# A recommender forward pass: the token sum and the comparison constant move into a PSUM bank, and the table sums into one bank with pairs that end at step ends

## Chip, cores, metric

The kernel runs on one core of one Trainium2 chip. The metric is device time in microseconds (us), lower is better. In the profile PE is TensorE's matmuls, PEld its weight loads, DVE is VectorE, ACT is ScalarE, POOL is GpSimd.

## What is computed

```python
tok = word_emb[token_idx].mean(axis=1)        # (16384, 32) indices, 50000 x 300 table
e1 = emb_mh1[mh1_idx].mean(axis=1)            # 20 indices each; 1000, 5000, 10000 rows x 64
e2 = emb_mh2[mh2_idx].mean(axis=1)
e3 = emb_mh3[mh3_idx].mean(axis=1)
o1, o2, o3, o4 = emb_oh1[oh1_idx], ...        # one index each; 100, 50, 20, 1000 rows
emb = concatenate([tok, e1, e2, e3, o1, o2, o3, o4], axis=1)      # 748 columns
wide = sums of one-column tables at the same small-table indices
h = relu(emb @ W1 + b1)                       # 1024
h = relu(h @ W2 + b2)                         # 512
h = relu(h @ W3 + b3)                         # 256
return sigmoid(h @ Wd + bd + wide)
```

All data is f32; the batch is 16384.

## The kernel before

The batch is cut into 128 tiles of 128 examples; four tiles make a block of 512, on which the layers run (the last four tiles form blocks of two, one and one). A tile passes through three pieces of work, and the loop at L454 writes their order out by hand, in 11 steps (STEPS) per tile, with the program's own order kept on each engine.

**Tokens** (L212). For each of 32 tokens GpSimd issues one indirect DMA (a gather) that brings 128 rows of 300 f32 values into SBUF. Four gathers make a group; the ring holds three groups. One group later (TOK_LAG) `add_up` (L204) has VectorE reduce the four rows and the running sum, five rows of 300, to the next group's running sum or, at the end of the tile, to the feature tile g.

**Small tables** (L281 to L345). The rows of the seven small tables lie in SBUF as three bf16 terms, in 138 slices of 128 rows. A lookup becomes a count matrix: VectorE compares the row number and the slice number of each lookup with the constant `iota` (`one_hots`, L289, two comparisons a step, for six examples of each half, in the last step four), TensorE multiplies the two one-hot matrices into counts (`counts`, L307, 12 small matmuls into pc), and ScalarE writes them to cnt as fp8 (L314). In the next tile's steps `small_sums` multiplies cnt by the terms, 138 matmuls of 195 columns into pg (L332), two tables to a pg tile, four such pairs; after each pair VectorE reduces the three terms into g (L339). pg has two PSUM buffers.

**Layers** (L367 to L419). For a whole block TensorE transposes the features in six chunks (L374), VectorE scales them into x (L375), and 88 f32 matmuls (L384) with ScalarE's relu (L393) make the three layers; then the output row (L409, L413, L417). This runs beside the next block's tiles.

Each piece is a generator. `Paced` (L421) takes an equal part of its units in each step: the sums a part of 138 + LULL units, the layers a part of a block's units over the next block's steps, a chunk of transposes counting two (CHUNK_WORK) and a matmul one. Within a step the order is: comparisons of the next step, counts, tokens, table sums, layers. The key transposes (L272, L275) come once a block. In the first tile the tables are converted to bf16 terms (L154 to L172), by ScalarE and by VectorE's L169.

Of the kernel before, what the change touches and what calls it, by code (L numbers as in the profile page):

```python
# [8 lines left out]
F32 = mybir.dt.float32  # L9
# [10 lines left out]
N_MH, EMB = 20, 64  # L20
ROW = EMB + 1
D1, D2, D3 = 1024, 512, 256
TOK_GROUP = 4
TOK_LAG = 1
TOK_RING = 3
BLOCK = 512
HALF = P // 2
N_SMALL = 3 * N_MH + 4
ONEHOT = 6
STEPS = -(-HALF // ONEHOT)  # L30
LULL = 12
CHUNK_WORK = 2

# [11 lines left out]
def kernel(  # L47
# [31 lines left out]
        slices[f] = (n_h, n_h + n)  # L79
        n_h += n  # L80

    tokp = ctx.enter_context(tc.tile_pool(name="tok", bufs=1))
    const = ctx.enter_context(tc.tile_pool(name="const", bufs=1))
    idxp = ctx.enter_context(tc.tile_pool(name="idx", bufs=2))
    keyp = ctx.enter_context(tc.tile_pool(name="keys", bufs=1))
# [5 lines left out]
    xp = ctx.enter_context(tc.tile_pool(name="x", bufs=1))  # L91
    ps_h = ctx.enter_context(tc.tile_pool(name="ps_h", bufs=2, space=bass.MemoryType.PSUM))
    ps_c = ctx.enter_context(tc.tile_pool(name="ps_c", bufs=1, space=bass.MemoryType.PSUM))
    ps_g = ctx.enter_context(tc.tile_pool(name="ps_g", bufs=2, space=bass.MemoryType.PSUM))

# [20 lines left out]
    nc.vector.memset(scale[0:EMB, 4:5], 1.0 / N_MH)  # L118


    iota_i = keyp.tile([P, n_h], I32, name="iota_i", tag="low")
    nc.gpsimd.iota(iota_i, pattern=[[1, n_h]], base=0, channel_multiplier=0)
    iota = const.tile([P, n_h], BF16, name="iota")
    nc.vector.tensor_copy(iota, iota_i)

    first = const.tile([P, 2, N_SMALL], I32, name="first")
    lookups = [("e1", N_MH), ("e2", N_MH), ("e3", N_MH), ("o1", 1), ("o2", 1), ("o3", 1), ("o4", 1)]
# [65 lines left out]
        for sb, dram in ((wd_sb, wd), (b1_sb, b1), (b2_sb, b2), (b3_sb, b3), (bd_sb, bd)):  # L193
            nc.sync.dma_start(out=sb, in_=dram)

    GROUP_ROWS = 1 + TOK_GROUP
    ring = tokp.tile([P, TOK_RING * GROUP_ROWS, TOK_D], F32, name="ring")
    n_groups = N_TOK // TOK_GROUP  # L200
    under_way = []
    features = {}

    def add_up(t, q):  # L204

        n = t * n_groups + q
        row, next_row = (k % TOK_RING * GROUP_ROWS for k in (n, n + 1))
        to = features[t][:, 0:TOK_D] if q == n_groups - 1 else ring[:, next_row, :]
        rows = ring[:, row + (q == 0) : row + GROUP_ROWS, :]
        nc.vector.tensor_reduce(to, rows.rearrange("p t d -> p d t"), AX.X, ALU.add)  # L210

    def tokens(t, it):  # L212


        for q in range(n_groups):
            row = 1 + (t * n_groups + q) % TOK_RING * GROUP_ROWS
            for r in range(TOK_GROUP):
                j = q * TOK_GROUP + r
                nc.gpsimd.indirect_dma_start(  # L219
                    out=ring[:, row + r, :],  # L220
                    out_offset=None,
                    in_=word,
                    in_offset=bass.IndirectOffsetOnAxis(ap=it[:, j : j + 1], axis=0),
                )
            under_way.append((t, q))
            if len(under_way) > TOK_LAG:
                add_up(*under_way.pop(0))
            yield 1
# [23 lines left out]
    def lookup_keys(ix):  # L252

        pairs = NSUB // 2
        low = keyp.tile([P, pairs, 2, N_SMALL], I32, name="low", tag="low")
        nc.vector.tensor_single_scalar(low, ix, P - 1, op=ALU.bitwise_and)
        nc.vector.tensor_single_scalar(ix, ix, 7, op=ALU.logical_shift_right)
        keys = keyp.tile([P, pairs, 2, 2 * N_SMALL], BF16, name="keys")
        for r in range(pairs):
            view = keys[:, r].rearrange("p w (f c) -> p w f c", f=2)  # L260
            nc.vector.tensor_copy(view[:, 0], low[:, r])
            nc.vector.tensor_add(view[:, 1], ix[:, r], first)
        return keys
# [58 lines left out]
    def small_sums(g, cnt):  # L322


        by_slice = cnt.rearrange("l f p h -> l (f p) h")
        for i in (0, 2, 6, 4):
            pair = SMALL[i : i + 2]
            pg = ps_g.tile([P, 2, 3 * ROW], F32, name="pg")
            for j, f in enumerate(pair):
                h0, h1 = slices[f]  # L330
                for h in range(h0, h1):
                    nc.tensor.matmul(  # L332
                        pg[:, j, :], by_slice[:, :, h], terms[:, h, :], start=(h == h0), stop=(h == h1 - 1)
                    )
                    if h < h1 - 1:
                        yield 1
            at = TOK_D + i * ROW
            n = len(pair)
            nc.vector.tensor_reduce(  # L339
                g[:, at : at + n * ROW].rearrange("p (f d) -> p f d", f=n),  # L340
                pg[:, 0:n, :].rearrange("p f (c d) -> p f d c", c=3),
                AX.X,
                ALU.add,
            )
            yield n if i != 6 else n + LULL  # L345

    def wide_term(g):
        wide = wp.tile([P, 1], F32, name="wide")
# [47 lines left out]
    def mlp(b0, gs, wides):  # L396

        n = len(wides) * P
        x = xp.tile([P, NK, BLOCK], F32, name="x", tag="even")
        yield from transposed(x, gs)  # L400
        h1 = xp.tile([P, M1, BLOCK], F32, name="h1", tag="odd")
        yield from layer(h1, w1_sb, b1_sb, x, chunk_k, M1, n)
        h2 = xp.tile([P, M2, BLOCK], F32, name="h2", tag="even")
        yield from layer(h2, w2_sb, b2_sb, h1, [P] * M1, M2, n)
        h3 = xp.tile([P, M3 + 1, BLOCK], F32, name="h3", tag="odd")
        yield from layer(h3, w3_sb, b3_sb, h2, [P] * M2, M3, n)
        po = ps_h.tile([1, BLOCK], F32, name="po", tag="ph")
        for k in range(M3):
            nc.tensor.matmul(  # L409
                po[:, 0:n], wd_sb[:, k : k + 1], h3[:, k, 0:n], start=(k == 0), stop=False  # L410
            )
        for s, wide in enumerate(wides):
            nc.tensor.matmul(  # L413
                po[:, s * P : (s + 1) * P], wide, ident, start=False, stop=(s == len(wides) - 1)
            )
        y = h3[0:1, M3, 0:n]
        nc.scalar.activation(y, po[:, 0:n], AF.Sigmoid, bias=bd_sb)  # L417
        nc.sync.dma_start(out=out[b0 : b0 + n, :].rearrange("n o -> o n"), in_=y)
        yield M3  # L419

    class Paced:  # L421


        def __init__(self, gen, size, n):
            self.gen, self.size, self.n = gen, size, n
            self.done = self.part = 0

        def go(self):
            self.part += 1
            while self.done * self.n < self.size * self.part:  # L430
                work = next(self.gen, None)
                if work is None:
                    return
                self.done += work

        def finish(self):
            for _ in self.gen:
                pass

    tiles = B // P
    mlp_size = NK * (CHUNK_WORK + M1) + M1 * M2 + M2 * M3 + M3
    ctx.enter_context(tc.manual_schedule())
    sizes = [NSUB] * (tiles // NSUB - 1) + [NSUB - 2, 1, 1]
    it, ix = load_indices(0)
# [5 lines left out]
    for t in range(tiles + 1):  # L454
        s = t % NSUB
        sums = None
        if before:
            features[t - 1] = g = gp.tile([P, G_COLS], F32, name="g")
            sums = Paced(small_sums(g, before), n_h + LULL, STEPS)
        if t < tiles:  # L460
            if s == 0 and t:
                it, sc = next_it, next_sc
            cnt = cp.tile([P, 2, HALF, n_h], FP8, name="cnt", tag="counts")
            toks = Paced(tokens(t, it[:, s, :].bitcast(U32)), n_groups, STEPS)
        else:
            last_tokens()
        for i in range(STEPS):
            if t < tiles:
                hot_now = hot
                if s == 1 and i == 0 and t + NSUB < tiles:  # L470
                    next_it, ix = load_indices(t // NSUB + 1)
                if s == 2 and i == 0 and t + NSUB < tiles + 1:
                    next_keys = lookup_keys(ix)
                if i < STEPS - 1:
                    hot = one_hots(sc, s, i + 1)
                elif t + 1 < tiles:
                    hot = one_hots(next_sc if s == NSUB - 1 else sc, (s + 1) % NSUB, 0)
                counts(cnt, hot_now, i)
                if t == 0 and i % 3:
                    next(tables_on_chip, None)  # L480
                if t == 0 and i == STEPS - 1:
                    load_weights()
                toks.go()
            if s == 2 and i == 1 and t + NSUB < tiles + 1:
                next_sc = key_columns(next_keys)
            if sums:
                sums.go()
            if layers:
                layers.go()
        if before:  # L490
            sums.finish()
            gs.append(g)
            wides.append(wide_term(g))
        before = cnt if t < tiles else None
        if t == 0:
            for _ in tables_on_chip:
                pass
        if len(gs) == sizes[0]:
            if layers:
                layers.finish()  # L500
            steps = STEPS * (sizes[1] if len(sizes) > 1 else 1)
            layers = Paced(mlp(b0, gs, wides), mlp_size, steps)
            b0 += len(gs) * P
            gs, wides, sizes = [], [], sizes[1:]
    layers.finish()
# [39 lines left out]
```

## Time and profile before

| | us |
|---|---|
| median of 3 timed runs | 5522.64 (5520.22 to 5526.17) |
| the profiled execution | 5520.13 |
| its span | 5518.2 |
| TensorE matmul busy | 5127.8 |
| VectorE busy | 4677.3 |
| GpSimd busy | 4111.8 |
| ScalarE busy | 2544.8 |

The span is the time from the first to the last instruction of the profiled execution. A group's row gives line, engine, operation, output and inputs with shapes, count, then busy us, mean ns of one, and the idle time of the engine just before these instructions with what ended most of it. A row of the timeline gives start, duration, engine, line, operation and, in brackets, the idle time before it and what ended it; in the chain of waits a row is start, length, engine, tile, line and count.

### The profile page before, as it was taken

Reading aid. Unit: us, or ns where it says so; the run is one execution under the profiler, and the core shown is the slowest. Engines: PE = TensorE matmul, PEld = TensorE weight load, DVE = VectorE, ACT = ScalarE, POOL = GpSimd, SP = SyncE. Lnnn points to the kernel's source line nnn. Section 1 sums busy time; section 2 is a strip of 40 time slices with the busy share of each in tenths; the row PEclk is TensorE's granted clock in tenths of the full one; section 3 lists DMA queues with packets and bytes.
Section 4 is the critical chain, followed back from the end, with each engine's and each line's share of the span. In section 5 each row is a group of like instructions: output and inputs, shape, how many; then the busy total and the mean of one; then the engine's idle time right before and its main releaser. Section 6 shows DMA issues by size and latency. Waiting matters only on the chain.

```text
span 5518.2 us, 98099 instructions
## 1 busy us (share of the span) xinstructions
PE 5127.8 (93%) x41320; PEld 3192.2 (58%) x41320; DVE 4677.3 (85%) x5069; ACT 2544.8 (46%) x2000; POOL 4111.8 (75%) x4103
## 2 busy tenths in 40 slices
PE   3699999999999999999999999999999999999999
PEld 2555555555555555556555555555565555565558
DVE  7888888888888888888888888888888888888863
ACT  4344444444444444444444444444444444444443
POOL 5777777777777777777777777777777777777762
PEclk9799999999999999999999999999999999999999
DMA  5444444444444444444444444444444444444431
GB/s 161 118 120 118 121 118 120 122 118 119 121 120 121 121 119 119 121 119 121 120 120 121 119 120 121 120 119 120 121 119 122 119 119 120 120 121 120 119 97 36
DMA packets 245306, 652.21 MB, mean 118 GB/s; under 512 B 108977, under 2 KB 111988, under 8 KB 244863
## 3 DMA queue, kind: packets, MB, share of 16 engines
q0 software_dynamic: 196608, 629.41, 41.5%
q1 hardware_dynamic: 48255, 16.53, 1.3%
q8 instruction: 323, 5.29, 0.4%
q14 instruction: 120, 0.98, 0.1%
HBM read 645.59 MB, written 0.07 MB: 117 GB/s over the span
## 4 chain that ended last, share of the span: by engine, by line
PE 63%; POOL 12%; DVE 11%; issue 10%; DMA 4%; DVEq 0%; ACT 0%; POOLq 0%
PE ph L384 33%; PE pg L332 21%; POOL ring L219 12%; PE pc L307 8%; DMA ring<-in_word_emb_dram,it 4%; DVE ring L210 4%; DVE row L289 2%; DVE slice L289 1%; DVE x L375 1%; PE po L409 1%; DVE g L339 1%; DVE sc L275 1%; DVE g L210 1%; PE po L413 0%; PE pt L374 0%
## 5 line engine op out<-in xcount | busy, mean ns | idle before, releaser
L219 POOL DMA_INDIRECT ring<-in_word_emb_dram,it x4096 | 4110.9, 1004 | 1320.3 <-issue 1118.9
L314 ACT ACTIVATE cnt<-pc 128x1656 fp8e3<-128x1656 f32 (+1 forms) x1408 | 2121.8, 1507 | 2232.7 <-PE pc L307 2208.4
L210 DVE TENSOR_REDUCE ring<-ring 128x300 f32<-128x1500 f32 (+1 forms) x896 | 2510.2, 2802 | 207.8 <-DMA ring<-in_word_emb_dram,it 205.2
L332 PE MATMUL pg<-terms,cnt 128*128 128x195 bf16 x17664 | 1874.9, 256 | 93.4 <-DVE g L339 93.4
L332 PEld LDWEIGHTS <-cnt 128*128 128x128 fp8e3 x17664 | 1614.6, 145 | 251.8 <-issue 101.6
L384 PE MATMUL ph<-x,w_sb 128*128 128x512 f32 (+5 forms) x3264 | 1470.7, 580 | 42.2 <-DVE sc L275 41.8
L384 PE MATMUL ph<-h,w_sb 128*128 128x512 f32 (+2 forms) x2720 | 1204.5, 572 | 0.0
L307 PEld LDWEIGHTS <-row 64*128 64x128 bf16 x16384 | 511.0, 96 | 1191.3 <-issue 487.3
L289 DVE TENSOR_TENSOR row<-iota,sc 128x768 bf16<-128x768 bf16 (+1 forms) x1408 | 760.4, 540 | 344.3 <-PE pc L307 337.5
L307 PE MATMUL pc<-slice,row 64*128 64x138 bf16 x16384 | 768.9, 226 | 241.5 <-DVE slice L289 203.8
L384 PEld LDWEIGHTS ph<-x,w_sb 128*128 128x128 f32 (+1 forms) x3264 | 555.1, 191 | 462.2 <-issue 391.9
L289 DVE TENSOR_TENSOR slice<-iota,sc 128x828 bf16<-128x828 bf16 (+1 forms) x1408 | 805.3, 572 | 0.0
L384 PEld LDWEIGHTS ph<-h,w_sb 128*128 128x128 f32 x2720 | 464.1, 191 | 346.6 <-issue 344.7
L393 ACT ACTIVATE h<-ph,b_sb 128x512 f32<-128x512 f32 (+2 forms) x476 | 315.2, 662 | 700.7 <-PE ph L384 697.3
L339 DVE TENSOR_REDUCE g<-pg 128x130 f32<-128x390 f32 (+1 forms) x512 | 249.4, 508 | 208.5 <-PE pg L332 208.3
L210 DVE TENSOR_REDUCE g<-ring 128x300 f32<-128x1500 f32 x128 | 374.7, 2927 | 0.0
L375 DVE TENSOR_SCALAR x<-pt,scale 128x512 f32<-128x512 f32 (+4 forms) x204 | 143.0, 716 | 17.7 <-PE pt L374 17.0
L374 PE MATMUL pt<-ident,g 128*128 128x128 f32 (+1 forms) x768 | 113.4, 275 | 2.9 <-DVE x L375 2.4
L374 PEld LDWEIGHTS pt<-ident,g 128*128 128x128 f32 (+1 forms) x768 | 86.1, 141 | 5.7 <-DVE x L375 5.0
L409 PE MATMUL po<-h,wd_sb 128*1 128x512 f32 (+2 forms) x136 | 60.9, 566 | 0.3
L314 ACT ACT_TABLE_LOAD x32 | 41.1, 1283 | 1.3 <-PEq L530 0.7
L417 ACT ACT_TABLE_LOAD x32 | 41.1, 1283 | 0.6
(31 smaller groups left out, 290.9 us busy)
## 6 DMA issues: line engine op xcount, KB each, us to landing
ring<-in_word_emb_dram,it POOLq DMA_INDIRECT x4096
ix<-in_idx_dram SPq DMA_DIRECT2D x128, 32.0 KB
w_sb<-in_W_dram SPq DMA_DIRECT2D x6, 512.0 KB
it<-in_idx_dram SPq DMA_DIRECT2D x32, 64.0 KB
w_sb<-in_W_dram SPq DMA_DIRECT2D x1, 2048.0 KB
raw<-in_mh_dram SPq DMA_DIRECT2D x1, 975.0 KB
out_dram<-h SPq DMA_DIRECT2D x31, 2.0 KB
raw<-in_mh_dram SPq DMA_DIRECT2D x1, 292.5 KB
```

What stands on the lines that cost most here:

```text
L210: nc.vector.tensor_reduce(to, rows.rearrange("p t d -> p d t"), AX.X, ALU.add)
L219: nc.gpsimd.indirect_dma_start(out=ring[:, row + r, :], out_offset=None, in_=word, in_offset=bass.IndirectOffsetOnAxis(ap=it[:, j : j + 1] ...
L289: nc.vector.tensor_tensor(one[:, 0:rows, :].rearrange("p i (n d) -> p i n d", d=2), iota[:, 0:n].rearrange("p (n d) -> p n d", d=2).unsque ...
L307: nc.tensor.matmul(pc[:, f, k // n, at : at + n_h], hot[0][half, k, :], hot[1][half, k, :], start=True, stop=True,)
L314: nc.scalar.activation(cnt[:, :, b : b + rows, :].rearrange("l f (g k) h -> l f g (k h)", g=2), pc[:, :, :, 0 : n * n_h], AF.Copy, scale=0 ...
L332: nc.tensor.matmul(pg[:, j, :], by_slice[:, :, h], terms[:, h, :], start=(h == h0), stop=(h == h1 - 1))
L339: nc.vector.tensor_reduce(g[:, at : at + n * ROW].rearrange("p (f d) -> p f d", f=n), pg[:, 0:n, :].rearrange("p f (c d) -> p f d c", c=3) ...
L374: nc.tensor.transpose(pt[:kk, s * P : (s + 1) * P], chunk(g, k), ident)
L375: nc.vector.tensor_scalar(x[:kk, k, 0:n], pt[:kk, 0:n], scale[:kk, k : k + 1], None, ALU.mult)
L384: nc.tensor.matmul(ph[:, 0:n], weights[:kk, k, m * P : (m + 1) * P], src[:kk, k, 0:n], start=(k == 0), stop=(k == len(kks) - 1),)
L393: nc.scalar.activation(dst[:, m, 0:n], ph[:, 0:n], AF.Relu, bias=bias[:, m : m + 1])
L409: nc.tensor.matmul(po[:, 0:n], wd_sb[:, k : k + 1], h3[:, k, 0:n], start=(k == 0), stop=False)
```

## The change

It does six things.

1. A PSUM tile `own` of one bank, which VectorE alone uses, holds `iota` (bf16 values, written as f32 words) and the running token sum. The comparisons read `iota` from there.
2. A token group is two gathers in a tile of its own from a pool of six; three groups later VectorE adds the two rows to the sum in PSUM, one `tensor_add` a row (the first add of a tile takes both rows; the last writes g).
3. pg has one buffer in place of two.
4. The pairs of tables come in the order 0, 2, 4, 6; `sums_by_step` cuts the sums so that pairs end in steps 0, 8, 9 and 10 of a tile and at most one ends in a step. LULL goes.
5. A chunk of transposes counts one unit in place of two.
6. The layers get what the sums leave of an equal share of each step, one layer unit counted as ten table matmuls (LAYER_TIME).

```diff
-TOK_GROUP = 4
-TOK_LAG = 1
-TOK_RING = 3
+TOK_GROUP = 2
+TOK_LAG = 3
...
-LULL = 12
-CHUNK_WORK = 2
+CHUNK_WORK = 1
+LAYER_TIME = 10
...
-    tokp = ctx.enter_context(tc.tile_pool(name="tok", bufs=1))
+    tokp = ctx.enter_context(tc.tile_pool(name="tok", bufs=2 * TOK_LAG))
...
-    ps_g = ctx.enter_context(tc.tile_pool(name="ps_g", bufs=2, space=bass.MemoryType.PSUM))
+    ps_g = ctx.enter_context(tc.tile_pool(name="ps_g", bufs=1, space=bass.MemoryType.PSUM))
+    ps_v = ctx.enter_context(tc.tile_pool(name="ps_v", bufs=1, space=bass.MemoryType.PSUM))
...
+    own = ps_v.tile([P, 512], F32, name="own")
+    tok_sum = own[:, 128 : 128 + TOK_D]
...
-    iota = const.tile([P, n_h], BF16, name="iota")
-    nc.vector.tensor_copy(iota, iota_i)
+    iota_s = keyp.tile([P, n_h], BF16, name="iota_s", tag="keys")
+    nc.vector.tensor_copy(iota_s, iota_i)
+    nc.vector.tensor_copy(own[:, 0 : n_h // 2], iota_s.bitcast(F32))
+    iota = own[:, 0 : n_h // 2].bitcast(BF16)
...
-    def add_up(t, q):
-
-        n = t * n_groups + q
-        row, next_row = (k % TOK_RING * GROUP_ROWS for k in (n, n + 1))
-        to = features[t][:, 0:TOK_D] if q == n_groups - 1 else ring[:, next_row, :]
-        rows = ring[:, row + (q == 0) : row + GROUP_ROWS, :]
-        nc.vector.tensor_reduce(to, rows.rearrange("p t d -> p d t"), AX.X, ALU.add)
+    def add_up(t, q, rows):
+
+        a, b = rows[:, 0:TOK_D], rows[:, TOK_D : 2 * TOK_D]
+        if q == 0:
+            nc.vector.tensor_add(tok_sum, a, b)
+        else:
+            nc.vector.tensor_add(tok_sum, tok_sum, a)
+            to = features[t][:, 0:TOK_D] if q == n_groups - 1 else tok_sum
+            nc.vector.tensor_add(to, tok_sum, b)
...
-        for i in (0, 2, 6, 4):
+        for i in (0, 2, 4, 6):
...
-                    if h < h1 - 1:
-                        yield 1
+                    yield 1
...
-            yield n if i != 6 else n + LULL
+            yield None
...
+    def sums_by_step(gen):
+
+
+
+        done, n_pairs = 0, 4
+        n_first = slices["e1"][1] - slices["o4"][0]
+        n_second = slices["e3"][1] - slices["e2"][0]
+        for i in range(STEPS):
+
+            steps = STEPS - (n_pairs - 1)
+            upto = n_first + -(-n_second * i // steps)
+            for work in gen:
+                if work is None:
+                    break
+                done += work
+                if n_first < done < n_first + n_second and done == upto:
+                    break
+            yield done
...
-    mlp_size = NK * (CHUNK_WORK + M1) + M1 * M2 + M2 * M3 + M3
+    mlp_time = (NK * (CHUNK_WORK + M1) + M1 * M2 + M2 * M3 + M3) * LAYER_TIME
...
-            if sums:
-                sums.go()
+            done = next(sums) if sums else 0
             if layers:
-                layers.go()
+                share = (n_h + layers_time) * (i + 1) / STEPS - done
+                layers.to((layers_before + share) / LAYER_TIME)
...
-            steps = STEPS * (sizes[1] if len(sizes) > 1 else 1)
-            layers = Paced(mlp(b0, gs, wides), mlp_size, steps)
+            layers = Paced(mlp(b0, gs, wides))
+            layers_time, layers_before = mlp_time / (sizes[1] if len(sizes) > 1 else 1), 0
```

More of the change, by code (lines that the diff above doesn't have):

```diff
@@ L194, in load_weights @@
             nc.sync.dma_start(out=sb, in_=dram)
-    GROUP_ROWS = 1 + TOK_GROUP
-    ring = tokp.tile([P, TOK_RING * GROUP_ROWS, TOK_D], F32, name="ring")
     n_groups = N_TOK // TOK_GROUP
@@ L202 @@
     features = {}
-    def add_up(t, q):
-        n = t * n_groups + q
-        row, next_row = (k % TOK_RING * GROUP_ROWS for k in (n, n + 1))
-        to = features[t][:, 0:TOK_D] if q == n_groups - 1 else ring[:, next_row, :]
-        rows = ring[:, row + (q == 0) : row + GROUP_ROWS, :]
-        nc.vector.tensor_reduce(to, rows.rearrange("p t d -> p d t"), AX.X, ALU.add)
+    def add_up(t, q, rows):
[6 more added lines that the diff above has]
+            nc.vector.tensor_add(to, tok_sum, b)
     def tokens(t, it):
         for q in range(n_groups):
-            row = 1 + (t * n_groups + q) % TOK_RING * GROUP_ROWS
+            rows = tokp.tile([P, TOK_GROUP * TOK_D], F32, name="tok_rows")
             for r in range(TOK_GROUP):
@@ L219, in tokens @@
                 nc.gpsimd.indirect_dma_start(
-                    out=ring[:, row + r, :],
+                    out=rows[:, r * TOK_D : (r + 1) * TOK_D],
                     out_offset=None,
@@ L224, in tokens @@
                 )
-            under_way.append((t, q))
+            under_way.append((t, q, rows))
             if len(under_way) > TOK_LAG:
@@ L257, in lookup_keys @@
         nc.vector.tensor_single_scalar(ix, ix, 7, op=ALU.logical_shift_right)
-        keys = keyp.tile([P, pairs, 2, 2 * N_SMALL], BF16, name="keys")
+        keys = keyp.tile([P, pairs, 2, 2 * N_SMALL], BF16, name="keys", tag="keys")
         for r in range(pairs):
@@ L421, with __init__, to @@
     class Paced:
[L424 to L430, printed above, removed]
+        def __init__(self, gen):
+            self.gen, self.done = gen, 0
+        def to(self, size):
+            while self.done < size:
                 work = next(self.gen, None)
@@ L458 @@
             features[t - 1] = g = gp.tile([P, G_COLS], F32, name="g")
-            sums = Paced(small_sums(g, before), n_h + LULL, STEPS)
+            sums = sums_by_step(small_sums(g, before))
         if t < tiles:
@@ L463 @@
             cnt = cp.tile([P, 2, HALF, n_h], FP8, name="cnt", tag="counts")
-            toks = Paced(tokens(t, it[:, s, :].bitcast(U32)), n_groups, STEPS)
+            toks = Paced(tokens(t, it[:, s, :].bitcast(U32)))
         else:
@@ L482 @@
                     load_weights()
-                toks.go()
+                toks.to(n_groups * (i + 1) / STEPS)
             if s == 2 and i == 1 and t + NSUB < tiles + 1:
                 next_sc = key_columns(next_keys)
-            if sums:
-                sums.go()
+            done = next(sums) if sums else 0
             if layers:
-                layers.go()
+                share = (n_h + layers_time) * (i + 1) / STEPS - done
+                layers.to((layers_before + share) / LAYER_TIME)
+        if layers:
+            layers_before += layers_time
         if before:
-            sums.finish()
+            assert done == n_h and next(sums, None) is None
             gs.append(g)
```

## Prediction

> **What bounds the kernel now.** I read the page first, then GpSimd (POOL) alone between 79 and 5311 us, then the timeline and the chain of waits around 2700 us. The page:
>
> ```profile
> span 5518.2 us, 98099 instructions
> ...
> PE 5127.8 (93%) x41320; PEld 3192.2 (58%) x41320; DVE 4677.3 (85%) x5069; ACT 2544.8 (46%) x2000; POOL 4111.8 (75%) x4103
> ```
>
> By these shares TensorE (PE) is the bound and GpSimd is not. The groups of GpSimd, its line's spread of durations, and the engines' busy time in the same stretch say otherwise:
>
> ```profile
> L219 POOL DMA_INDIRECT ring<-in_word_emb_dram,it x4000 | 4013.1, 1003 | 1229.1 <-issue 1095.5 <-DVE ring L210 41.0 <-DVE row L289 30.5
> ```
> ```profile
> L219 POOL DMA_INDIRECT ring<-in_word_emb_dram,it x4000: 942/946/2623, 79.2 to 5310.2; - x191
> ```
> ```profile
> 79.24 1.24 POOL L219 DMA_INDIRECT ring<-in_word_emb_dram,it  x1 [10.24 <-DVE ring L210]
> ```
> ```profile
> 79.00:5311.00 5232.00, 4915.93 (x39737) 3036.94 (x39738) 4537.06 (x4896) 2434.15 (x1887) 4012.93 (x4000) 0.98 0.44 120
> 5311.00:5518.00 207.00, 202.30 (x1461) 148.60 (x1460) 90.22 (x108) 68.83 (x86) 63.65 (x65) 1.00 0.18 50
> ```
>
> The 4000 gathers of tiles 1 to 125 take 4013.1 us. Of the idle 1229.1 us, 10.2 lie before the first; the rest is 0.305 us for each, which the timeline shows between any two gathers. Together that fills the stretch: GpSimd issues gathers without a pause for 125 tiles, 32 x (1.003 + 0.305) = 41.9 us a tile. That, not TensorE, sets the pace until 5311 us. After it TensorE is busy 202 of 207 us (columns: PE, PEld, DVE, ACT, POOL, clock, DMA, GB/s): the last layers, which the change leaves.
>
> The median gather is 0.946 us, the mean 1.003. The timeline shows which are long:
>
> ```profile
> 2704.13 2.87 DVE L210 TENSOR_REDUCE ring<-ring 128x300 f32<-128x1500 f32 x1
> ...
> 2704.83 0.95 POOL L219 DMA_INDIRECT ring<-in_word_emb_dram,it  x1 [0.30 <-issue]
> ...
> 2711.01 0.56 DVE L289 TENSOR_TENSOR row<-iota,sc 128x768 bf16<-128x768 bf16 x1 [3.05 <-PE pc L307]
> 2711.08 1.31 POOL L219 DMA_INDIRECT ring<-in_word_emb_dram,it  x1 [0.30 <-issue]
> ```
> ```profile
> 27.44 1.72 DVE L169 SCALAR_TENSOR_TENSOR raw<-raw,terms 128x1495 f32<-128x1495 f32 x1 [1.25 <-ACT terms L167]
> 28.06 1.92 POOL L219 DMA_INDIRECT ring<-in_word_emb_dram,it  x1 [0.30 <-issue]
> ```
>
> A gather under the token reduction (one SBUF input) takes 0.95 us; one beside a comparison (two SBUF inputs, iota and sc) 1.31; one beside the f32 operation of L169, also with two SBUF inputs, 1.92. So what stretches gathers is a VectorE (DVE) operation with two SBUF inputs, whatever its type.
>
> How a late gather reaches TensorE:
>
> ```profile
> 2800.91 2.83 DVE L210 TENSOR_REDUCE ring<-ring 128x300 f32<-128x1500 f32 x1 [3.32 <-DMA ring<-in_word_emb_dram,it]
> ...
> 2804.27 0.33 PE L332 MATMUL pg<-terms,cnt 128*128 128x195 bf16 x2 [2.53 <-DVE g L339]
> ```
>
> VectorE waits 3.32 us for the rows; the reduction of pg is queued behind that wait, and TensorE waits 2.53 us for its bank.
>
> **The change part by part.** The profiled execution took 5520.1 us: span 5518.2 and 1.9 around it. That is 0.05% under the median of the three timed runs, 5522.6.
>
> *iota in PSUM.* Each comparison then has one SBUF input. If the stretch goes, a gather falls to the median: 4000 x (1003 - 946) ns = 228 us off the stretch from 79 to 5311 us.
>
> *What can still stretch a gather.* The first add of a tile has both rows in SBUF. The 2 x 1408 comparisons cost some 4096 x 57 ns = 233 us, 83 ns each of about 0.55 us; an add of 0.5 us then costs some 75 ns, 125 x 75 ns = 9 us. It cannot cost more than its own length, 63 us. Gathers per tile: 32 x 1.251 + 0.08 = 40.1 us.
>
> *Token sums.* Eight reductions a tile become 31 adds of 300 elements. The rows for their price:
>
> ```profile
> L210 DVE TENSOR_REDUCE ring<-ring 128x300 f32<-128x1500 f32 (+1 forms) x896 | 2510.2, 2802 | 207.8 <-DMA ring<-in_word_emb_dram,it 205.2
> ...
> L210 DVE TENSOR_REDUCE g<-ring 128x300 f32<-128x1500 f32 x128 | 374.7, 2927 | 0.0
> ```
> ```profile
> L289 DVE TENSOR_TENSOR slice<-iota,sc 128x828 bf16<-128x828 bf16 x1280 | 749.0, 585 | 0.0
> L289 DVE TENSOR_TENSOR row<-iota,sc 128x768 bf16<-128x768 bf16 x1280 | 706.6, 552 | 301.8 <-PE pc L307 295.0 <-issue 4.6 <-PE ph L384 1.2
> ...
> L339 DVE TENSOR_REDUCE g<-pg 128x130 f32<-128x390 f32 x384 | 215.1, 560 | 208.5 <-PE pg L332 208.3
> ...
> L289 DVE TENSOR_TENSOR row<-iota,sc 128x512 bf16<-128x512 bf16 x128 | 53.7, 420 | 42.5 <-PE pc L307 42.5
> L339 DVE TENSOR_REDUCE g<-pg 128x65 f32<-128x195 f32 x128 | 44.9, 351 | 0.0
> ```
> ```profile
> 2763.64 0.16 DVE L350 TENSOR_REDUCE wide<-g 128x1 f32<-128x6 f32 x1
> 2763.83 0.16 DVE L356 TENSOR_TENSOR wide<-wide,g 128x1 f32<-128x1 f32 x1
> ```
>
> The reductions go: (2510.2 + 374.7) / 128 = 22.5 us a tile. The two shapes of L339, which read PSUM, give (560 - 351) / 195 = 1.07 ns an element and 142 ns fixed, so 0.46 us for an add; each needs the one before, and L356 starts 0.03 us after the end of L350. I take 0.50 us. Below 0.46 nothing speaks for it; a second PSUM access at another fixed part makes 0.64. 31 x 0.50 = 15.5 us (14.3 to 19.8).
>
> *Comparisons.* Now (552 - 420) / 256 = 0.52 ns an element, twice as fast as L339. No row has a bf16 operation with two inputs, one in PSUM. Ends: unchanged (no reason for a gain: as many elements, same pattern), or 1.07 ns an element, 0.96 and 1.03 us, 0.86 us more a step, 9.1 us a tile (10.67 full steps). I take unchanged, as type, pattern and count of each operand stay as in the nearest row, L289 itself. The Trainium skill is of two minds. "VectorE: DVE Perf Modes", in its perf-mode tier table, gives tensor_tensor with any PSUM operand one element per cycle, which would be the upper end (rival B). "Vector Engine (DVE) Microarchitecture Reference", section 5.1, makes the two-at-a-time mode depend on 2-byte types and unit steps, not on the memory, which would be the lower.
>
> *VectorE's load.* Now 4537 / 125 = 36.3 us a tile. Then 36.3 - 22.5 + 15.5 = 29.3 us of 40.1: not the bound.
>
> *TensorE.* The chain of waits around 2700 us is all TensorE and gives its true pace:
>
> ```profile
> 2707.89 2.60 PE ph L384 x6
> 2710.50 0.47 PE pc L307 x12
> 2710.97 1.37 PE pg L332 x14
> 2712.34 1.74 PE ph L384 x4
> ...
> 2763.00 1.81 PE po L409 x4
> 2764.81 0.87 PE po L413 x8
> ```
> ```profile
> 2767.45 1.03 PE L374 MATMUL pt<-ident,g 128*128 128x128 f32 x8
> ...
> 2779.39 0.54 PE L307 MATMUL pc<-slice,row 64*128 64x138 bf16 x12 [2.13 <-DVE slice L289]
> ```
>
> ```profile
> L384 PE MATMUL ph<-x,w_sb 128*128 128x512 f32 (+5 forms) x3264 | 1470.7, 580 | 42.2 <-DVE sc L275 41.8
> L384 PE MATMUL ph<-h,w_sb 128*128 128x512 f32 (+2 forms) x2720 | 1204.5, 572 | 0.0
> ```
>
> The layers run 34 times, (3264 + 2720) / 34 = 176 records each, two for every f32 matmul, 0.435 us a record: a unit of the pacing is 0.87 us. Per block of four tiles: counts 4 x 10.67 x 0.47 = 20.1, table sums 4 x 138 x 0.098 = 54.1, layers 176 x 0.435 = 76.6, transposes 24 x 0.13 = 3.1, output 2.7: 156.6 us. Gathers: 4 x 40.1 = 160.4. So TensorE, not far behind, is what is late next. The old pacing gives every tile 102 / 4 = 25.5 units, a chunk of transposes counted as two: a tile without chunks then needs 18.5 + 25.5 x 0.87 = 40.7 us, over 40.1. The new one counts a chunk as one: 24 units, 39.4 us, under it, and spreads them over steps of equal weight.
>
> ```profile
> 2768.16 1.41 DVE L375 TENSOR_SCALAR x<-pt,scale 128x512 f32<-128x512 f32 x2 [0.34 <-PE pt L374]
> ```
> ```profile
> L272 PE MATMUL pk<-ident_bf,keys 128*128 128x128 bf16 x128 | 13.4, 227 | 7.5 <-DVE keys L261 7.4
> ```
> ```profile
> PEld po L409 <- ACT h L393: 12.6, 34, 0.8
> ```
>
> The tile with chunks has two in each of steps 0 to 2. VectorE's load there: comparisons 1.05, adds 31 / 11 x 0.5 = 1.4, two scaled copies 1.4, in step 0 a reduction 0.56: 4.4, 3.9, 3.9 against 40.1 / 11 = 3.65 a step. TensorE has some 2.9 us of work in such a step, so it loses 0.75 x 3, and 1.25 us to VectorE's lag, 3.5 us (now, too, it waits there: 2.13 us above); key transposes and the wait in the output layer add 13.4 / 32 + 12.6 / 32 = 0.8: 160.9 a block, 0.5 over the gathers, 31 x 0.5 = 16 us.
>
> *One pg bank.* A pair's first sum waits for the reduction of the pair before. Pairs now end at steps 0, 8, 9 and 10, with layers (1.74) and counts (0.47) between; 2.2 us hide a 0.56 us reduction. I take nothing. Queued behind the reduction's wait on VectorE are scaled copies and the comparisons of the step after next, needed a whole step later. Without that cover it is 3 x 0.56 + 0.35 = 2.0 us a tile, 250 us.
>
> *Three groups of two.* VectorE at a group's place waited for rows 4 gathers back, now 6 back; room stays 12 rows, so gathers and steps may drift apart as far as before. As many gathers go on the same queue. The first tile, 79 us against 42 of the others, waits for the sums and the table conversion; shorter sums save a few us, I take 4. The set-up copies of iota run once.
>
> Sum: 5520 - 228 + 9 + 16 - 4 = 5313.
>
> **The rivals.**
> B. The comparisons fall to one element at a time: VectorE 38.4 us of 40.1. It idles 41.9 - 36.3 = 5.6 us a tile now, waiting for TensorE and rows; if half of that stays, 41.2 us a tile: 5520 - 125 x 0.7 = 5435. For it: the PSUM rows L339; against: those are reductions in f32.
> C. The stretch stays: the gather is held by something other than the second SBUF input, such as VectorE's writes. Then 41.9 us a tile stays and the time is 5520, the lighter VectorE worth nothing. Against it: L210 writes SBUF too and stretches nothing. The Trainium skill leans to C at one place: "SBUF — State Buffer", Who interferes with whom, infers that tensor_tensor spares descriptor generation; the 1.31 us row contradicts it.
> D. Slower: VectorE becomes the bound through PSUM latency, comparisons at 1.07 ns an element and adds at 0.64: 36.3 - 22.5 + 19.8 + 9.1 = 42.7 us a tile, 125 x 0.8 = 100 us more, 5620. It decides from 41.9 us of VectorE on, that is, with slow comparisons, from 0.61 us an add. Against it: two unknowns at their worst ends at once.
>
> **How the numbers follow.** Forecast 0.73, B 0.10, C 0.09, D 0.08. About 0.2%, 11 us, is what a measurement here can tell from no change. Forecast and B are faster, and a little of C: 0.84; same 0.08, the rest of C; slower 0.08. The forecast's own range is 5270 (TensorE never late, 16 us, and the first tile shorter by 30) to 5375 (adds at 0.64, 1.2 us more a block in the chunk steps, and pg's bank at a tenth of its price). To hold eight in ten it must reach over B: 5270 to 5445.
>
> **What would show it.** Right: gathers with mean near 0.95 us, the stretch of 125 tiles near 5010 to 5040 us, adds near 0.5, comparisons still 0.55 to 0.6, TensorE at 97% or more. Comparisons near 1 us mean B or D; a mean gather near 1.0 with comparisons unchanged means C; many waits of pg sums on its reduction mean that the single bank is not covered.

## The result, and the profile after

| | us |
|---|---|
| before, median of 4 runs | 5521.43 (5518.58 to 5526.17) |
| changed, median of 4 runs | 5285.88 (5284.62 to 5287.96) |
| ratio, 95% interval | 0.9573 (0.9556 to 0.959) |
| forecast | 5313 (5270 to 5445) |
| the profiled execution, its span | 5285.83, 5284.0 |

The changed kernel is 4.3% faster. The page's first rows show shares only, as they did before:

```profile
span 5284.0 us, 104301 instructions
...
PE 5073.1 (96%) x41320; PEld 3160.4 (60%) x41320; DVE 3763.4 (71%) x8014; ACT 2528.4 (48%) x2000; POOL 3881.2 (73%) x4103
```

GpSimd's share went down, 75 to 73%, and it is still what sets the pace. The same two views as before, GpSimd's group over tiles 1 to 125 (now 78 to 5083 us) and the engines' busy time, say so:

```profile
L223 POOL DMA_INDIRECT tok_rows<-in_word_emb_dram,it x4002 | 3787.8, 946 | 1219.2 <-issue 734.1 <-DVE own L214 306.2 <-DVE own L212 52.7
```
```profile
79.00:5090.00 5011.00, 4874.35 (x39814) 3012.22 (x39815) 3647.69 (x7775) 2421.99 (x1890) 3789.12 (x4004) 0.99 0.46 125
```

The gather's mean is now the 946 ns that was its median, and idle time is again 1219.2 / 4002 = 0.305 us for each, nothing more. The names behind the idle time (DVE own L214) are only the semaphore that happened to come last before one of those 0.305 us gaps; were they real waits, the sum would be over 0.305 a gather. A tile takes 32 x (0.946 + 0.305) = 40.0 us where it took 41.9. TensorE is busy 4874 of 5011 us, 97.3%: it has 1.1 us a tile to spare.

The rows that were without a neighbour in the trace of before, the comparisons and the adds:

```profile
L212 DVE TENSOR_TENSOR own<-own,tok_rows 128x300 f32<-128x300 f32 x1875 | 897.0, 478 | 399.0 <-DMA tok_rows<-in_word_emb_dram,it 348.6
...
L293 DVE TENSOR_TENSOR slice<-own,sc 128x828 bf16<-128x828 bf16 x1250 | 723.4, 579 | 0.0
L293 DVE TENSOR_TENSOR row<-own,sc 128x768 bf16<-128x768 bf16 x1250 | 691.8, 553 | 117.7 <-PE pc L311 43.6 <-DVE own L214 3.7 <-PE ph L387 0.5
```

A comparison with iota in PSUM takes 553 and 579 ns; in SBUF it took 552 and 585. An add takes 478 ns.

Where the 234 us of span went, by the start of the first gather of tiles 1 and 126: tile 0 from 79.2 to 78.4 us (1 less), tiles 1 to 125 from 5235.8 to 5004.5 us (231 less), the rest from 203 to 201 us (2 less).

Five of the experiments below were first run where the kernel before itself took 7387 or 7524 us, at a granted clock of 0.88 in place of 0.98; those times (iota_sbuf 7169, sum_sbuf 7214, iota_only 7898, old_pacing 7528 us against 7524, ring_kept 7510 against 7387) are left out of the argument, and the second run of each, with _2 behind its name, was made where the kernel before takes 5520 us.

### The profile page after: what moved, and what is told of

Read it like the earlier page. It is cut to its first block, busy times and chain, and to the rows that moved or that the text cites. A ratio compares the mean times of both kernels' runs of the same rounds, so it can differ in the third digit from the quotient of the medians.

```text
span 5284.0 us, 104301 instructions
## 1 busy us (share of the span) xinstructions
PE 5073.1 (96%) x41320; PEld 3160.4 (60%) x41320; DVE 3763.4 (71%) x8014; ACT 2528.4 (48%) x2000; POOL 3881.2 (73%) x4103
## 4 chain that ended last, share of the span: by engine, by line
PE 26%; DMA 26%; issue 17%; DVE 17%; POOL 12%; ACT 1%; SPq 0%; DVEq 0%; POOLq 0%; ACTq 0%
DMA tok_rows<-in_word_emb_dram,it 25%; PE ph L387 14%; POOL tok_rows L223 12%; PE pg L336 8%; DVE own L214 5%; DVE own L212 3%; PE pc L311 3%; DVE slice L293 3%; DVE row L293 1%; DVE x L378 1%; DVE g L342 1%; DVE own L210 1%; PE po L412 1%; DMA raw<-in_mh_dram 0%; ACT cnt L318 0%
## 5 line engine op out<-in xcount | busy, mean ns | idle before, releaser
L223 POOL DMA_INDIRECT tok_rows<-in_word_emb_dram,it x4096 | 3880.3, 947 | 1324.0 <-issue 754.2
L336 PE MATMUL pg<-terms,cnt 128*128 128x195 bf16 x17664 | 1847.6, 254 | 83.1 <-DVE g L342 81.4
L214 DVE TENSOR_TENSOR own<-own,tok_rows 128x300 f32<-128x300 f32 x1792 | 857.1, 478 | 715.5 <-DMA tok_rows<-in_word_emb_dram,it 684.8
L212 DVE TENSOR_TENSOR own<-own,tok_rows 128x300 f32<-128x300 f32 x1920 | 918.5, 478 | 400.3 <-DMA tok_rows<-in_word_emb_dram,it 348.6
L293 DVE TENSOR_TENSOR row<-own,sc 128x768 bf16<-128x768 bf16 (+1 forms) x1408 | 761.3, 541 | 156.5 <-PE pc L311 81.7
L293 DVE TENSOR_TENSOR slice<-own,sc 128x828 bf16<-128x828 bf16 (+1 forms) x1408 | 796.2, 565 | 0.0
L210 DVE TENSOR_TENSOR own<-tok_rows 128x300 f32<-128x300 f32 x128 | 61.5, 480 | 47.5 <-DMA tok_rows<-in_word_emb_dram,it 44.6
L214 DVE TENSOR_TENSOR g<-own,tok_rows 128x300 f32<-128x300 f32 x128 | 60.2, 470 | 25.9 <-DMA tok_rows<-in_word_emb_dram,it 21.1
```

What stands on the lines that cost most here:

```text
L212: nc.vector.tensor_add(tok_sum, tok_sum, a)
L214: nc.vector.tensor_add(to, tok_sum, b)
L223: nc.gpsimd.indirect_dma_start(out=rows[:, r * TOK_D : (r + 1) * TOK_D], out_offset=None, in_=word, in_offset=bass.IndirectOffsetOnAxis(ap ...
L293: nc.vector.tensor_tensor(one[:, 0:rows, :].rearrange("p i (n d) -> p i n d", d=2), iota[:, 0:n].rearrange("p (n d) -> p n d", d=2).unsque ...
L336: nc.tensor.matmul(pg[:, j, :], by_slice[:, :, h], terms[:, h, :], start=(h == h0), stop=(h == h1 - 1))
```

## The experiments

Theory 1: a VectorE operation with two SBUF inputs stretches the gathers, and the gathers pace the kernel, as long as TensorE and VectorE keep up. Rival 2: the gain comes from the lighter VectorE (31 adds for eight reductions). Rival 3: it comes from the even pacing of TensorE. Rival 4, a cost: the single pg bank.

**iota back in SBUF** (iota_sbuf, iota_sbuf_2), the rest of the change kept:

```diff
-    nc.vector.tensor_copy(own[:, 0 : n_h // 2], iota_s.bitcast(F32))
-    iota = own[:, 0 : n_h // 2].bitcast(BF16)
+    iota = const.tile([P, n_h], BF16, name="iota")
+    nc.vector.tensor_copy(iota, iota_s)
```

> The changed kernel with iota back in SBUF, all else of the change kept. Theory 1 (a VectorE operation with two SBUF inputs stretches the gathers, and the gathers pace the kernel): 22 comparisons a tile stretch again by 83 ns each, mean gather near 1.003 us, 41.9 us a tile, 5286 + 229 = 5515 us. Rival 2 (the gain comes from the lighter VectorE, adds for reductions) and rival 3 (it comes from the even pacing of TensorE): both stay as they are, near 5290 us.

> Again the changed kernel with iota back in SBUF, on another chip, because on the first one the kernel before itself took 7500 us. Theory 1: the 22 comparisons of a tile stretch the gathers by 83 ns each, mean gather 1.003 us; GpSimd issues without a pause, 32 x (1.003 + 0.305) = 41.9 us a tile, 5286 + 229 = 5515 us. On the first chip the mean was 0.980 us with GpSimd waiting a quarter of the time, so fewer gathers met a comparison; with no waits it should be near 1.003. Rivals 2 and 3 (lighter VectorE, even pacing): near 5290 us.

Measured 5420.7 us, ratio to before 0.9815 (0.9798 to 0.9831): between the theories. Its gathers:

```profile
L223 POOL DMA_INDIRECT tok_rows<-in_word_emb_dram,it x3999 | 3919.6, 980 | 1218.5 <-issue 723.4 <-DVE own L214 326.0 <-DVE own L212 36.0
```

Idle time is again 0.305 us a gather, so GpSimd never waits, and 32 x (0.980 + 0.305) = 41.1 us a tile gives the time. The stretch came back, by 34 ns a gather and not 57: with 22 comparisons to 32 gathers that is 50 ns a comparison, not 83. The mechanism held, the fixed price did not. Rivals 2 and 3, which said 5290, fall as the whole cause; that 100 us of the gain stay with iota in SBUF is taken up under pacing_only.

**The running sum in SBUF** (sum_sbuf, sum_sbuf_2), iota in PSUM:

```diff
-    tok_sum = own[:, 128 : 128 + TOK_D]
+    tok_sum = const.tile([P, TOK_D], F32, name="tok_sum")
```

> The changed kernel with the running token sum in SBUF and iota in PSUM. Theory 1: 31 adds a tile then have two SBUF inputs and stretch gathers by some 75 ns each, 2.3 us a tile, 125 tiles: 290 us more, 5575 us, mean gather near 1.02 us. Rivals 2 and 3: VectorE's load and the pacing are unchanged, near 5290 us.

> Again the changed kernel with the running token sum in SBUF, iota in PSUM, on a chip where the kernel before takes 5520 us. Theory 1 with the prediction's price, 75 ns an add: 31 x 75 ns = 2.3 us a tile, mean gather 1.02 us, 5575 us. With the stretch seen on the first chip (mean 0.973 us, GpSimd often waiting): 32 x 0.027 = 0.9 us a tile, 5395 us or, as GpSimd then never waits, somewhat more. Without any stretch by adds (the second input is not the cause): 5290 us.

Measured 5353.4 us, ratio 0.9693 (0.9677 to 0.971).

```profile
L223 POOL DMA_INDIRECT tok_rows<-in_word_emb_dram,it x3999 | 3854.3, 964 | 1218.2 <-issue 754.9 <-DVE tok_sum L214 290.9 <-DVE tok_sum L212 39.3
```

The adds, now with two SBUF inputs, stretch gathers as well, by 18 ns a gather: 18 x 32 / 31 = 19 ns an add, a quarter of the price I had put on it. The run takes 68 us more than with the sum in PSUM; without a stretch by adds it would have been 5290. The adds' output moves to SBUF with their input here; but the reductions write to SBUF as well and stretch nothing (ring_kept_2, below).

**iota in PSUM alone, in the kernel before** (iota_only, iota_only_2). The bank has to come from pg:

```diff
-    ps_g = ctx.enter_context(tc.tile_pool(name="ps_g", bufs=2, space=bass.MemoryType.PSUM))
+    ps_g = ctx.enter_context(tc.tile_pool(name="ps_g", bufs=1, space=bass.MemoryType.PSUM))
+    ps_v = ctx.enter_context(tc.tile_pool(name="ps_v", bufs=1, space=bass.MemoryType.PSUM))
...
-    iota = const.tile([P, n_h], BF16, name="iota")
-    nc.vector.tensor_copy(iota, iota_i)
+    nc.vector.tensor_copy(own[:, 0 : n_h // 2], iota_s.bitcast(F32))
+    iota = own[:, 0 : n_h // 2].bitcast(BF16)
```

> The kernel before with iota alone in PSUM; for its bank pg goes from two buffers to one; reductions, ring and pacing as before. Theory 1 alone: gathers at 0.947 us, and if nothing else is late 40.0 us a tile, near 5290 us. Rival 2: VectorE keeps 36.3 us of work a tile, now of 40.0, and makes TensorE late: 5350 to 5450 us. Rival 3: tiles without transposes need 40.7 us of TensorE: some 0.7 us on three tiles of four, 5350 us. The single bank without pairs at step ends may add up to 2 us a tile, 5540 us.

> Again the kernel before with iota alone in PSUM and one pg buffer, on a chip where the kernel before takes 5520 us. Theory 1: gathers at 0.946 us without a pause, 40.0 us a tile, near 5290 us. Rival 2 (VectorE's 36.3 us of work in 40.0 makes TensorE late): 5350 to 5450 us, with GpSimd waiting for the ring. Rival 4, the single bank without pairs at step ends: up to 2 us a tile, 5540 us, with long waits of pg sums on its reduction.

Measured 5975.6 us, ratio 1.0815 (1.0797 to 1.0833): outside every expectation. GpSimd's group between 77 and 277 us (the layers start at 245 us), and from 79 to 5700 us:

```profile
L223 POOL DMA_INDIRECT ring<-in_word_emb_dram,it x158 | 149.4, 946 | 58.7 <-issue 39.9 <-DVE ring L214 13.6 <-DVE row L293 1.8
```
```profile
L223 POOL DMA_INDIRECT ring<-in_word_emb_dram,it x3964 | 3747.7, 945 | 1883.6 <-issue 1049.5 <-DVE g L214 399.0 <-DVE ring L214 377.9
```

The gathers are unstretched, 945 ns. In the first stretch the idle time is the 0.305 us each plus 10 before the first, 40 us a tile, as theory 1 has it. With the layers the idle time grows to 0.475 a gather, and now the names count: GpSimd waits for the ring. Who holds the ring is in the waits (us in total, times, the longest), and in one place of VectorE's and TensorE's timelines:

```profile
PE pg L336 <- DVE g L343: 506.3, 256, 5.6
POOL ring L223 <- DVE ring L214: 449.0, 239, 10.2
```
```profile
3013.99 2.94 DVE L214 TENSOR_REDUCE ring<-ring 128x300 f32<-128x1500 f32 x1
3016.81 0.58 DVE L343 TENSOR_REDUCE g<-pg 128x130 f32<-128x390 f32 x1
```
```profile
3017.45 0.24 PE L336 MATMUL pg<-terms,cnt 128*128 128x195 bf16 x1 [2.21 <-DVE g L343]
```

A pair ended in the middle of a step; its reduction stood behind a token reduction of 2.94 us, and TensorE, with the next pair first in its order, stood 2.21 us. Such waits come to 506 us. That all else the run lost follows from them is not shown: against ring_kept_2 below, which differs in the pacing and the order of the pairs alone, TensorE is also busy 234 us longer (5308.8 against 5074.6).

**The old pacing in the changed kernel** (old_pacing, old_pacing_2): constants, order of pairs and `Paced` as before; iota, token sum and the single pg bank as in the change.

```diff
-        for i in (0, 2, 4, 6):
+        for i in (0, 2, 6, 4):
...
-            sums = sums_by_step(small_sums(g, before))
+            sums = Paced(small_sums(g, before), n_h + LULL, STEPS)
...
-                layers.to((layers_before + share) / LAYER_TIME)
+                layers.go()
```

> The changed kernel with the pacing of before: pairs in the order 0, 2, 6, 4 with the lull, ending anywhere in a step, a chunk counted two, layers paced by themselves; pg still has one buffer, iota and the token sum are in PSUM. Theory 1: the gathers pace it, near 5290 us. Rival 3: 40.7 us on three tiles of four, and waits of pg sums on its reduction up to 2 us a tile: 5350 to 5540 us.

> Again the changed kernel with the old pacing and order of pairs, pg in one buffer. Theory 1 alone: near 5290 us, gathers 0.946 us without a pause. Rivals 3 and 4 (40.7 us of TensorE on three tiles of four; waits of pg sums on its reduction): 5350 to 5540 us, with GpSimd waiting for VectorE's adds.

Measured 5637.0 us, ratio 1.0204 (1.0187 to 1.0221): 351 us over the changed kernel, slower than before.

```profile
PE pg L336 <- DVE g L343: 306.1, 260, 5.2
```

```profile
L223 POOL DMA_INDIRECT tok_rows<-in_word_emb_dram,it x3984 | 3771.2, 947 | 1550.6 <-issue 862.6 <-DVE own L214 361.7 <-DVE own L212 102.0
```

The gathers take 947 ns, and GpSimd's idle time is 0.389 us each: it waits. TensorE waits 306 us for pg's reduction, where the changed kernel's page has 81:

```profile
L336 PE MATMUL pg<-terms,cnt 128*128 128x195 bf16 x17664 | 1847.6, 254 | 83.1 <-DVE g L342 81.4
```

So the new pacing does not shorten a gather; it pays for the bank. TensorE's idle time grows by 229 us, nearly all of it these waits, and its busy time by 124 us (5197.3 against 5073.1), for which I have no cause. This run also brings back the uneven tiles together with the pairs; which share is whose was not tried. Against iota_only_2 the tokens' part of the change (adds of 0.48 us in front of a reduction of pg, in place of 2.9) saves 339 us; with the new pacing it saves 5, next run.

**Ring and reductions kept in the changed kernel** (ring_kept, ring_kept_2):

```diff
-            nc.vector.tensor_add(tok_sum, tok_sum, a)
-            to = features[t][:, 0:TOK_D] if q == n_groups - 1 else tok_sum
-            nc.vector.tensor_add(to, tok_sum, b)
+        rows = ring[:, row + (q == 0) : row + GROUP_ROWS, :]
+        nc.vector.tensor_reduce(to, rows.rearrange("p t d -> p d t"), AX.X, ALU.add)
```

> The changed kernel with the token ring and the reductions of before; iota in PSUM, one pg buffer and the new pacing stay. Theory 1 (gathers of 0.946 us, unstretched, pace the kernel): no operation here has two SBUF inputs in the tokens either, 40.0 us a tile, 5290 us. Rival 2 (the lighter VectorE carries the gain): VectorE keeps 36.3 us of work in 40.0 a tile, and steps with two chunks of transposes fall behind by 2 us more: 5340 to 5400 us.

> Again the changed kernel with the ring and the reductions of before. Theory 1: 40.0 us a tile, 5290 us. Rival 2: VectorE's 36.3 us of work in 40.0 makes TensorE late in the steps with transposes, 5340 to 5400 us, GpSimd waits for the ring.

Measured 5291.3 us, ratio 0.958 (0.9564 to 0.9596).

```profile
L224 POOL DMA_INDIRECT ring<-in_word_emb_dram,it x4000 | 3782.4, 946 | 1230.5 <-issue 1078.7 <-DVE ring L215 106.2 <-DMA ring<-in_word_emb_dram,it 18.9
```

Rival 2 falls for good: with VectorE as heavy as before the time is that of the changed kernel within 6 us.

**Pacing and one bank alone** (pacing_only): the run above with iota in SBUF, too, so that VectorE has nothing in PSUM.

```diff
-    ps_v = ctx.enter_context(tc.tile_pool(name="ps_v", bufs=1, space=bass.MemoryType.PSUM))
...
-    nc.vector.tensor_copy(own[:, 0 : n_h // 2], iota_s.bitcast(F32))
-    iota = own[:, 0 : n_h // 2].bitcast(BF16)
+    iota = const.tile([P, n_h], BF16, name="iota")
+    nc.vector.tensor_copy(iota, iota_s)
```

> The kernel before with the new pacing and one pg buffer, and nothing of VectorE's in PSUM: iota, ring and reductions as before. Theory 1 with a fixed price (each comparison stretches by 83 ns, as before): mean gather 1.003 us, 41.9 us a tile, 5515 us. If the price hangs on where in a gather the comparisons fall (with iota in SBUF but adds for the tokens the mean was 0.981 us): reductions as before put them where they were before, so 1.00 us and 5500 us again, and the adds were what moved them; were it the pacing that moved them, 0.98 us and 5420 us. Rival 3 (even pacing carries the gain): 5290 us.

Measured 5572.9 us, ratio 1.0082 (1.0061 to 1.0103).

```profile
L221 POOL DMA_INDIRECT ring<-in_word_emb_dram,it x4000 | 4077.2, 1019 | 1229.1 <-issue 1031.1 <-DVE row L291 60.3 <-DVE ring L212 56.2
```

Rival 3 falls: even pacing without PSUM is slower than before, because the gathers are stretched more, 73 ns each, 106 ns a comparison. Against ring_kept_2 only the place of iota differs: its move to PSUM takes 282 us off. Waits for pg's reduction need not cost time, either: TensorE has 227 us of them here, and GpSimd does not wait for one.

The same 22 comparisons cost 83 ns in the kernel before, 106 here and 50 with adds. So adds in place of reductions cut the stretch (152 us between pacing_only and iota_sbuf_2), and the price depends on what stands around the comparisons. The traces show on what. The prediction's comparison at 2711.01 us ends at 2711.57, and the gather that began under it ends 0.82 us later, at 2712.39; the operation of L169 ends at 29.16, and its gather 0.82 us later, at 29.98. A comparison that begins after the gather leaves it alone, here in the kernel before:

```profile
2796.41 0.95 POOL L219 DMA_INDIRECT ring<-in_word_emb_dram,it  x1 [0.30 <-issue]
...
2796.83 0.40 DVE L289 TENSOR_TENSOR row<-iota,sc 128x512 bf16<-128x512 bf16 x1
```

And with iota in PSUM a gather that begins under a comparison keeps its length, here in iota_only_2:

```profile
3018.01 0.55 DVE L293 TENSOR_TENSOR row<-own,sc 128x768 bf16<-128x768 bf16 x1
...
3018.16 0.95 POOL L223 DMA_INDIRECT ring<-in_word_emb_dram,it  x1 [0.30 <-issue]
```

Counted over the 4000 gathers of tiles 1 to 125 in each trace, "begun under" meaning that a comparison (in sum_sbuf_2 an add) is under way as the gather begins and has more than 0.13 us left:

| run | inputs in SBUF | gathers begun under | of these over 0.96 us | their time over 0.946 us each, us | that of all 4000, us |
|---|---|---|---|---|---|
| before | two | 872 | 811 | 225 | 229 |
| pacing_only | two | 921 | 872 | 269 | 293 |
| iota_sbuf_2 | two | 805 | 676 | 133 | 136 |
| sum_sbuf_2 | two | 579 | 513 | 72 | 71 |
| ring_kept_2 | one | 907 | 0 | 0 | -2 |

Of the 872 of the kernel before, 674 end 0.82 us after that comparison ends and 136 as long after a later one ends, within 0.015 us; of the 1038 gathers there that only meet a comparison begun after them, 10 are over 0.96 us. So a price for each comparison is a mean: what counts is how many gathers begin under one, and how much of it, and of what follows it, is left. With adds (iota_sbuf_2) fewer begin so than in pacing_only, and fewer, 28 against 126, are held by a later comparison, too. What in the gather has to wait the traces do not show.

**The table conversion of the first tile reordered** (start_up), in the changed kernel. In place of one chunk after another, four chunks in turn, VectorE's subtraction two operations behind ScalarE's, two operations a step:

```diff
-                for c in range(3):
...
-                    nc.scalar.activation(term, rows, AF.Copy, scale=scale)
-                    if c < 2:
-                        nc.vector.scalar_tensor_tensor(
-                            rows, rows, scale, term, op0=ALU.mult, op1=ALU.subtract
-                        )
...
+            for k, (c, raw, a, term) in enumerate(tasks):
+                subtract(k - 2)
+                nc.scalar.activation(
+                    term, raw[:, a : a + CHUNK, :], AF.Copy, scale=2.0 if c == 0 else 1.0
+                )
+                yield k
```

> The changed kernel with the table conversion of the first tile reordered: four chunks go round in turn, so that neither ScalarE nor VectorE waits for the other's last result, two operations a step. The first gather of the second tile started at 78.4 us, where 40 us of issuing would do. VectorE's own work in that tile is 11 x 1.05 + 15.5 + 12 x 1.72 = 48 us and starts at 10: if the waits go and the rest of the kernel runs 40.0 us a tile behind it, 20 us less, 5266 us. If what holds the first tile is the landing of the tables or the rows, no change, 5286 us.

Measured 5269.1 us, ratio 0.954 (0.9524 to 0.9556), 16.8 us under the changed kernel. Its group of gathers, 59 to 5061 us:

```profile
L242 POOL DMA_INDIRECT tok_rows<-in_word_emb_dram,it x3999 | 3785.2, 947 | 1218.3 <-issue 714.1 <-DVE own L233 312.6 <-DVE own L231 51.8
```

Tile 1 starts at 59.4 us in place of 78.4, and then the same 40.0 us a tile follow. What went are VectorE's waits for ScalarE in tile 0, 26.1 us in the changed kernel and 9.4 here, one subtraction of the twelve, which did not wait, lying outside the second row's stretch:

```profile
L175 DVE SCALAR_TENSOR_TENSOR raw<-raw,terms 128x1495 f32<-128x1495 f32 x12 | 20.6, 1717 | 26.1 <-ACT terms L173 26.1
```
```profile
L170 DVE SCALAR_TENSOR_TENSOR raw<-raw,terms 128x1495 f32<-128x1495 f32 x11 | 18.5, 1714 | 9.4 <-ACT terms L176 9.4
```

This version beats both kernels.

What the runs give together, 32 x (mean gather + 0.305) against the time:

| run | iota | token sum | mean gather, us | us a tile | time, us |
|---|---|---|---|---|---|
| before | SBUF | reductions | 1.003 | 41.9 | 5521 |
| pacing_only | SBUF | reductions | 1.019 | 42.4 | 5573 |
| iota_sbuf_2 | SBUF | adds in PSUM | 0.980 | 41.1 | 5421 |
| sum_sbuf_2 | PSUM | adds in SBUF | 0.964 | 40.6 | 5353 |
| ring_kept_2 | PSUM | reductions | 0.946 | 40.0 | 5291 |
| changed | PSUM | adds in PSUM | 0.946 | 40.0 | 5286 |

In these six GpSimd's pauses beyond the 0.305 us come to less than 4 us in tiles 1 to 125, and 125 x the tile + 282 us, fitted to the changed kernel, gives each time within 10 us. In the two runs with the old pacing and one bank it waits, and the row does not hold.

## Why the prediction was right

The mechanism was right and so was the place; the sum, 5313, was 27 us too high. For tiles 1 to 125 I had 228 - 9 - 16 = 203 us less, and 231 came: the two terms taken off were too large by 7 and 16. The stretch, 5004.5 us, so ended just under the 5010 to 5040 that I gave as a sign.

*The bound.* Right: GpSimd's gathers, not TensorE, set the pace, before and after.

*iota in PSUM.* Right in kind and size: 228 us forecast, and the 4000 gathers of tiles 1 to 125 took 227 us less. But what stretches a gather is not any operation beside it with two SBUF inputs: it has to be under way as the gather begins, which the rows I compared could not tell. So iota alone is worth 135 us beside adds (iota_sbuf_2) and 282 beside reductions with the new pacing (pacing_only); that the sum was right needs only that all of the stretch goes.

*The first add of a tile.* Mis-sized. I took 75 ns an add from the mean of the comparisons, 9 us in all. sum_sbuf_2 puts an add at 19 ns, which makes 125 x 19 ns = 2 us; in the changed kernel's trace 20 gathers begin under such an add, and they take 3 us more. The step that failed is one price for every operation with two SBUF inputs.

*Token sums.* An add at 0.50: right, 478 ns, the next one 0.51 us behind it in VectorE's timeline:

```profile
2646.46 0.48 DVE L212 TENSOR_TENSOR own<-own,tok_rows 128x300 f32<-128x300 f32 x1
2646.97 0.48 DVE L214 TENSOR_TENSOR own<-own,tok_rows 128x300 f32<-128x300 f32 x1
```

VectorE not the bound: right, 3648 us in 125 tiles, 29.2 a tile, forecast 29.3.

*Comparisons.* Unchanged: right. The trace decides between the two pages of the Trainium skill for this shape: "Vector Engine (DVE) Microarchitecture Reference", section 5.1, agrees, and the any-PSUM entry of the tier table in "VectorE: DVE Perf Modes" does not, with 553 ns for 768 elements.

*TensorE.* Its work was about right, 39.0 us a tile against 156.6 / 4 = 39.2; its loss was not there. I took 16 us for the steps with two chunks of transposes, on the reckoning that TensorE idles for the rest of a step of 3.65 us. The chunk steps of the changed kernel:

```profile
2641.07 0.54 PE L311 MATMUL pc<-slice,row 64*128 64x138 bf16 x12 [0.74 <-ACT cnt L318]
...
2643.87 0.55 PE L311 MATMUL pc<-slice,row 64*128 64x138 bf16 x12
...
2646.67 0.54 PE L311 MATMUL pc<-slice,row 64*128 64x138 bf16 x12
```

The counts follow each other after 2.80 us. A step is not 3.65 us long; that is the mean. Short steps can run ahead of the gathers, and the 12 rows of room, 15 us of gathers, hold the difference. Whatever TensorE waits costs nothing here, since no gather in tiles 1 to 125 starts more than 0.4 us after the one before it has ended.

*One pg bank.* Right that pairs at step ends hide it: 81 us of waits in all, none of them on the gathers' path. The price without cover, 250 us, was too low for what the runs undo: 351 us with the old pacing, and 684 with reductions in front as well (iota_only_2 against ring_kept_2). Both hold the uneven tiles, too, so that the bank's own share stays open; but I counted only pg's own reductions and not what stands before them on VectorE, as the 2.94 us at 3013.99 above.

*The first tile.* 4 us forecast, 1 found. There VectorE waits for ScalarE's conversion, as start_up showed, not for the sums.

*The rivals.* B did not come (its own sum gives 5432, not 5435): a comparison took 553 ns. C fell in the trace and again in two runs from both sides: two inputs in SBUF stretch, one does not. D's adds at 0.64 did not come either. That the change without its pacing ends slower than before, 2% by old_pacing_2, was in the text only as a cover's price; as a rival it would have been the better one of that side.

## What to carry to other kernels

An engine's busy share can hide that it issues without a pause: divide busy plus idle time by the count and see whether idle time is a fixed amount for each. If that engine is GpSimd with gathers, compare mean and median of the gather, and look for VectorE operations with two SBUF inputs that were under way as the long ones began; one operand in PSUM took the stretch away here. A PSUM bank taken from a double buffer had to be paid for here in the order of the work, so that the reduction that frees it has a whole step of other work beside it.

## What the runs showed of the hardware that was not expected

The stretch by an operation with two SBUF inputs is no constant: 106, 83 and 50 ns a comparison of the same shape in three kernels, 19 ns an add of 0.47 us. It falls on gathers that begin while the operation is under way: most of them (810 of 872 in the kernel before) end 0.82 us after it or one that follows it has ended. And a comparison of bf16 values with one operand in PSUM runs as fast as with both in SBUF, 553 against 552 ns for 768 elements.
